# Block 0 of a four-block transformer: the norm ahead of the second expert call, taken from one place behind the attention into pieces inside it

## The chip, the cores and the metric

The kernel runs on one core of a Trainium2 chip. The engines are named as in the profile: PE multiplies matrices, DVE and ACT work element by element, POOL issues the indirect transfers, SP issues the other transfers. The metric is the device time of one launch in microseconds (us); lower is better.

## The reference, cut to what matters

`x` has 4096 tokens of 128 numbers (16 batches of 256). Four blocks follow one another, each an expert or dense layer, an attention, and the same layer again. Only block 0 is touched by the change:

```
x = x + 0.5 * experts0(layernorm(x))
x = x + attention0(layernorm(x))        # causal linear attention, 16 heads of 8
x = x + 0.5 * experts0(layernorm(x))    # the second call
```

`attention0` maps q and k through `x + 1` or `exp(x)`, and takes for each token `sum(q.k v) / (sum(q.k) + 1e-6)` over the tokens up to it, then a projection and a bias. `experts0` sends each token to the one of eight experts whose router logit is highest, so every token's logits are needed before the first expert can start.

## The kernel before, in words

The tokens lie in 32 tiles of 128: tile `j` of `x`, of the normed `xn`, and of its transpose `xnT`. Batch `b` owns tiles `2b` and `2b + 1`.

**Attention of block 0** (`attn0`). A loop runs over the 16 batches `b` and over four groups of heads `g`. In each (b, g):

- `scores` multiplies keys with queries on PE (L665, two PSUM tiles of a pool of three), and DVE masks each result (L669);
- `values` of the group two places earlier multiplies the masked scores with the values on PE (L708, and the running state at L720), and ACT copies the sums from PSUM into `u` (L730);
- at g = 0 PE and DVE build the state (L689, L699), and `recips` of batch b - 2 (L600, L601) turns the sums of the denominators into reciprocals. It stores them and loads them back spread over rows (`a_rd`, `a_den`, L602 and L604);
- at g = 1 `sums_out` of batch b - 1 sends `u` to memory and loads the numerators and denominators back (`a_ud`, `a_num`, `a_dr`, L589 to L593);
- at g = 2 `divide` of batch b - 2 (L609), at g = 3 `project_out` of it: four matmuls on PE (L617, L618) and the addition into `x` on DVE (L620);
- in even batches, at g = 0, 1 and 2, `project` makes the keys, queries and values of the next pair of batches: a matmul (L636), two activations (L638, L640), one operation on DVE (L642) and transfers into the heads' rows (L541), and for the values four times a matmul (L649) and an addition (L650). `keys_turned` (L678, L680) transposes keys.

The sums, the projections, the state, the turned keys and the transposes of a norm share a PSUM pool of two slots (`pst`, `bufs=2`), used in turn in the order of the program. A slot is free when the engine that reads it is done.

Behind the loop come the last `values`, and then, in this order, `sums_out(15)`, `recips(14)`, `divide(14)`, `project_out(14)`, `recips(15)`, `divide(15)`, `project_out(15)`.

**Order.** `pin` ties an instruction to the pinned one before it on the same engine, so most of PE's, ACT's and DVE's order is that of the program text. What is not pinned (the additions into `x`, the features, `layernorm`) is placed by a scheduler between them. Each engine works through its order without overtaking.

**The norm of before.** `ffn0(1)` begins with `layernorm()`: two halves of 16 tiles. Each takes statistics on DVE (L272, L273), an exact reciprocal square root with one activation of ACT (L254 to L262), 16 operations on DVE that write `xn` (L279), transposes on PE (L282) and copies to `xnT` on ACT (L284). The scheduler moves the statistics of a batch to just behind its addition into `x`, and the rest of the first half into batches 10 and 11 of the attention. The second half comes after the last batch. `ffn0` then stores `xn` in four transfers (L333), makes the logits (L345) and routes from L347 on.

**The norm in pieces.** Later blocks use `norm_piece(c)`: four tiles' statistics, then the reciprocal square root in Newton steps on DVE (`roots`, L292 to L306), and four activations on ACT that write `xn` (L315). `turn_piece(c)` transposes four tiles on PE (L323) and copies them on ACT (L324). All of it is pinned.

Of the kernel before, what the change touches and what calls it, by code (L numbers as in the profile page):

```python
# [9 lines left out]
F32 = mybir.dt.float32  # L10
I32 = mybir.dt.int32
U32 = mybir.dt.uint32
AF = mybir.ActivationFunctionType
# [5 lines left out]
P = 128  # L19
# [6 lines left out]
LN_EPS = 1e-5  # L26
# [45 lines left out]
def macaron_kernel(ctx: ExitStack, tc: tile.TileContext, I: dict, out: bass.AP):  # L72
    nc = tc.nc
    V, S, PE, G, SP = nc.vector, nc.scalar, nc.tensor, nc.gpsimd, nc.sync
# [4 lines left out]
    small = ctx.enter_context(tc.tile_pool(name="small", bufs=2))  # L79
    dram = ctx.enter_context(tc.tile_pool(name="dram", bufs=1, space=DRAM))  # L80
    pst = Banks()


    x = main.tile([P, NT, D], F32, name="x")
# [152 lines left out]
    def pin(ins):  # L237

        e = ins.ins.engine
        if e in pinned:  # L240
            tc.add_manual_dep(
                ins.ins,
                pinned[e],
                mybir.DependencyInfo(mybir.DependencyClass.NoSync, mybir.DependencyReason.DATA),
                reason="order of the pipeline",
            )
        pinned[e] = ins.ins.name
        return ins
# [15 lines left out]
    def layernorm(halves=(0, 1)):  # L264

        half = NT // 2
        for h in halves:
            st = small.tile([P, half, 6], F32, tag="lnst", name="ln_st")
            mv = small.tile([P, half, 2], F32, tag="lnmv", name="ln_mv")
            rstd = small.tile([P, half], F32, tag="lnr", name="ln_rstd")  # L270
            for j in range(half):
                V.bn_stats(st[:, j, :], x[:, h * half + j, :])  # L272
                V.bn_aggr(mv[:, j, :], st[:, j, :])  # L273
            rsqrt(rstd, mv[:, :, 1], LN_EPS, half, "ln")
            for c in range(0, half, 4):
                tp = pst.tile([P, 512], F32, tag="tp", name="ln_tp")
                for i in range(4):
                    k, j = c + i, h * half + c + i
                    V.tensor_scalar(  # L279
                        xn[:, j, :], x[:, j, :], mv[:, k, 0:1], rstd[:, k : k + 1], ALU.subtract, ALU.mult  # L280
                    )
                    PE.transpose(tp[:, i * P : (i + 1) * P], xn[:, j, :], ident)  # L282
                j = h * half + c
                S.copy(xnT[:, j * P : (j + 4) * P], tp)  # L284

    def roots(src, eps):


        st = small.tile([P, 4, 6], F32, tag="pst", name="ln_st")
        mv = small.tile([P, 4, 2], F32, tag="pmv", name="ln_mv")  # L290
        for j in range(4):
            pin(V.bn_stats(st[:, j, :], src[:, j, :]))  # L292
        for j in range(4):
            pin(V.bn_aggr(mv[:, j, :], st[:, j, :]))
        v = small.tile([P, 4], F32, tag="pv", name="ln_v")
        pin(V.tensor_scalar(v, mv[:, :, 1], eps, None, ALU.add))
        r = small.tile([P, 4], F32, tag="pr", name="ln_r")
        pin(V.tensor_scalar(r.bitcast(I32), v.bitcast(I32), 1, None, ALU.logical_shift_right))
        pin(V.tensor_scalar(r.bitcast(I32), r.bitcast(I32), -1.0, float(0x5F3759DF), ALU.mult, ALU.add))
        w = small.tile([P, 4], F32, tag="pw", name="ln_w")  # L300
        for k in range(3):
            pin(V.scalar_tensor_tensor(w, r, -0.5, r, ALU.mult, ALU.mult))
            pin(V.tensor_tensor(w, w, v, ALU.mult))
            pin(V.scalar_tensor_tensor(r, w, 1.5, r, ALU.add, ALU.mult))
        less = small.tile([P, 4], F32, tag="pl", name="ln_less")
        pin(V.scalar_tensor_tensor(less, mv[:, :, 0], -1.0, r, ALU.mult, ALU.mult))  # L306
        return less, r

    def norm_piece(c):

        t0 = 4 * c
        less, r = roots(x[:, t0 : t0 + 4, :], LN_EPS)
        for j in range(4):
            pin(
                S.activation(  # L315
                    xn[:, t0 + j, :], x[:, t0 + j, :], AF.Identity, bias=less[:, j : j + 1], scale=r[:, j : j + 1]
                )
            )

    def turn_piece(c):  # L320
        tp = pst.tile([P, 512], F32, tag="tp", name="ln_tp")
        for i in range(4):
            pin(PE.transpose(tp[:, i * P : (i + 1) * P], xn[:, 4 * c + i, :], ident))  # L323
        pin(S.copy(xnT[:, c * 512 : (c + 1) * 512], tp))  # L324
# [2 lines left out]
        return xnT[:, j * P : (j + 1) * P]  # L327


    def ffn0(call):  # L330
        layernorm()
        for c in range(0, NT, 8):
            SP.dma_start(  # L333
                out=xn_dram[c * P : (c + 8) * P, :].rearrange("(j p) d -> p j d", p=P), in_=xn[:, c : c + 8, :]
# [1 line left out]
        with tc.tile_pool(name=f"f0r{call}", bufs=1) as rp, tc.tile_pool(name=f"f0w{call}", bufs=3) as wp, tc.tile_pool(  # L336
# [102 lines left out]
            n = B0 // P  # L439
# [183 lines left out]
    def attn0():  # L623
        with tc.tile_pool(name="a0", bufs=2) as ap, tc.tile_pool(name="a0k", bufs=1) as bp, tc.tile_pool(
# [116 lines left out]
            for b in range(BATCH):  # L741
                us[b] = ap.tile([P, NG, SEQ], F32, tag="u", name="a0_u")
                for g in range(NG):
                    aa[b, g] = scores(b, g)
                    if b == 1 and g == 0:
                        layernorm((1,))
                    if g > 1:
                        values(b, g - 2)
                    elif b:
                        values(b - 1, g + 2)  # L750
                    if g == 0:
                        state(b)
                        if b > 1:
                            H.recips(b - 2)
                    if g == 1 and b:
                        H.sums_out(b - 1, us.pop(b - 1))
                    if g == 2 and b + 1 < BATCH and b % 2 == 0:
                        keys_turned(b + 1)
                    if g == 2 and b > 1:
                        H.divide(b - 2)  # L760
                    if g == 3 and b > 1:
                        H.project_out(b - 2)
                    if b % 2 == 0 and g < 3:
                        project(b // 2 + 1, g)
                    if g == 2 and b + 1 < BATCH and b % 2:
                        keys_turned(b + 1)
# [2 lines left out]
            values(b, 3)  # L769
            H.sums_out(b, us.pop(b))  # L770
            H.recips(b - 1)
            H.divide(b - 1)
            H.project_out(b - 1)
            H.recips(b)
            H.divide(b)
            H.project_out(b)


    def attn3():
# [884 lines left out]
    def attn2():  # L1664

        NP2 = H2 // 2
        with tc.tile_pool(name="a2", bufs=2) as ap, tc.tile_pool(name="a2w", bufs=1) as wp, tc.tile_pool(
# [205 lines left out]
            def renorm(c):  # L1873

                r = held.pop("r")
                less, rs = roots(r, 1e-5)
                for j in range(4):
                    pin(S.activation(r[:, j, :], r[:, j, :], AF.Identity, bias=less[:, j : j + 1], scale=rs[:, j : j + 1]))
                xc = x[:, 4 * c : 4 * c + 4, :]
                G.tensor_tensor(xc, xc, bc(W["a2_beta"], 1, 4), ALU.add)  # L1880
                G.tensor_tensor(r, r, bc(W["a2_gamma"], 1, 4), ALU.mult)
                G.tensor_tensor(xc, xc, r, ALU.add)
# [46 lines left out]
    def ffn3(call, last):  # L1929
# [171 lines left out]
                    turn_piece(s - 5)  # L2101

    steps = [
        lambda: (ffn0(0), later_weights()), attn0, lambda: ffn0(1),
        lambda: ffn1(0, False), attn1, lambda: ffn1(1, True),
        lambda: ffn2(0), attn2, lambda: ffn2(1),
        lambda: ffn3(0, False), attn3, lambda: ffn3(1, True),
# [112 lines left out]
```

## Time and profile before

| | us |
|---|---|
| median of 3 runs | 2972.98 |
| lowest and highest | 2961.8, 2986.62 |
| the profiled execution | 2970.45 |
| its span | 2968.8 |
| PE busy in the span | 2325.6 (78%) |
| DVE busy | 1484.8 (50%) |
| ACT busy | 1056.7 (36%) |
| attention of block 0, from about 260 to 481: PE, DVE, ACT busy | 193.08, 141.29, 57.62 |
| from 481 to 514: PE, DVE, ACT busy | 21.33, 10.30, 6.43 |

The profile is one execution. A line of its timeline gives start and length in us, the engine, the line of the kernel, what is written from what, and in brackets how long the engine was idle before it and what released it. An engine that is idle costs nothing as long as what ends last doesn't wait for it.

### The profile page before, as it was taken

How to read it: one execution, taken by the hardware profiler on the slowest of the kernel's cores; microseconds unless marked ns; L12 is line 12 of the kernel's file. 1: busy time of each engine (PE TensorE's matmuls, PEld its weight loads, DVE VectorE, ACT ScalarE, POOL GpSimd, SP SyncE). 2: the span in 40 equal slices, each digit the busy share in tenths (PEclk: the TensorE clock that was granted, in tenths of full speed). 3: DMA queues.
4: the chain of work that ended last, by engine and by line, in shares of the span. 5: the costliest groups of instructions: out<-in, count | busy, mean ns of one | idle time of the engine just before them, and what ended most of it. 6: DMA issues, size and time to landing. Idle time of an engine off the chain costs nothing. (4 is left out here: it accounts for less than half of the span.)

```text
span 2968.8 us, 45435 instructions
## 1 busy us (share of the span) xinstructions
PE 2325.6 (78%) x16713; PEld 1708.1 (58%) x16713; DVE 1484.8 (50%) x4374; ACT 1056.7 (36%) x2383; POOL 766.6 (26%) x693
## 2 busy tenths in 40 slices
PE   5884987786465656268699995576999898999999
PEld 4773555675354545145466664453777655556877
DVE  5335664434437735732235556323455566654553
ACT  1222221122114412134445442243444355664443
POOL 1551000352461054167300100675111100003111
PEclk9997897797567866566899997577999989999999
DMA  4752232454341143445400002365000012210000
GB/s 142 242 163 48 86 98 69 124 162 135 78 97 54 43 107 73 137 119 142 124 1 8 5 12 71 88 146 122 1 1 1 9 46 53 71 58 12 11 8 11
DMA packets 207908, 221.13 MB, mean 74 GB/s; under 512 B 46265, under 2 KB 172938, under 8 KB 204306
## 3 DMA queue, kind: packets, MB, share of 16 engines
q1 hardware_dynamic: 171066, 179.80, 20.0%
q0 software_dynamic: 36608, 38.31, 7.4%
q8 instruction: 135, 2.21, 0.3%
q14 instruction: 99, 0.81, 0.1%
HBM read 145.88 MB, written 63.50 MB: 71 GB/s over the span
## 5 line engine op out<-in xcount | busy, mean ns | idle before, releaser
L315 ACT ACTIVATE xn<-x,ln_less,ln_r 128x128 f32<-128x128 f32 x288 | 118.6, 482 | 397.2 <-DVE ln_less L306 351.0
L482 PE MATMUL f_h<-f_xsT,f_w 128*128 128x256 f32 x736 | 193.9, 404 | 32.9 <-ACT f_sg L484 28.1
L837 DVE TENSOR_REDUCE a_nm<-a_s 128x4 f32<-128x1024 f32 x128 | 156.4, 1224 | 99.2 <-PE a_t L833 87.8
L1596 PE MATMUL f_h<-f_xgT,f_w 128*128 128x128 f32 x768 | 158.0, 369 | 38.7 <-DVE f_xgT L1590 29.1
L456 POOL DMA_INDIRECT f_xs<-xn_dram,f_src x92 | 90.7, 985 | 371.0 <-DVE f_past L429 290.0
L485 DVE SCALAR_TENSOR_TENSOR f_hs<-f_h,f_b1s,f_sg 128x256 f32<-128x256 f32 x184 | 88.1, 483 | 187.6 <-ACT f_sg L484 97.6
L841 ACT ACTIVATE a_e<-a_t 128x512 f32<-128x512 f32 x256 | 139.0, 594 | 97.2 <-PE a_t L833 97.2
L482 PEld LDWEIGHTS f_h<-f_xsT,f_w 128*128 128x128 f32 x736 | 137.2, 202 | 61.0 <-ACT f_sg L484 34.1
L1596 PEld LDWEIGHTS f_h<-f_xgT,f_w 128*128 128x128 f32 x768 | 134.5, 264 | 63.0 <-DVE f_xgT L1590 45.6
L1600 ACT ACTIVATE f_hs<-f_h,w_f_b 128x128 f32<-128x128 f32 x384 | 109.5, 368 | 171.8 <-PE f_h L1596 150.5
L833 PE MATMUL a_t<-a_q,a_k 32*128 32x256 f32 x1024 | 166.2, 408 | 4.6 <-ACT a_e L841 4.4
L323 PE MATMUL ln_tp<-ident,xn 128*128 128x128 f32 x288 | 66.1, 339 | 130.4 <-ACT xn L315 129.7
L1631 POOL DMA_INDIRECT acc<-f_ys,f_idx x96 | 151.8, 1581 | 46.9 <-DVE f_ys L1626 26.7
L484 ACT ACTIVATE f_sg<-f_h,f_b1s 128x256 f32<-128x256 f32 x184 | 84.7, 473 | 221.0 <-PE f_h L482 180.8
L833 PE MATMUL a_s<-a_k,a_q 32*128 32x256 f32 x1024 | 153.4, 426 | 2.3 <-DVE a_nm L837 1.6
L1626 DVE TENSOR_SCALAR f_ys<-f_up,f_xg,f_share 128x128 f32<-128x128 f32 x96 | 39.3, 410 | 189.4 <-PE f_up L1623 144.2
L2016 ACT ACTIVATE f_nh<-f_c,w_f_sh 128x256 f32<-128x256 f32 x192 | 87.0, 500 | 129.4 <-DVE f_c L2035 103.8
L323 PEld LDWEIGHTS ln_tp<-ident,xn 128*128 128x128 f32 x288 | 40.3, 160 | 157.8 <-ACT xn L315 144.8
L1154 POOL DMA_INDIRECT acc<-f_ys,f_idy x64 | 100.4, 1569 | 89.0 <-DVE f_ys L1150 63.7
L503 POOL DMA_INDIRECT yt_dram<-f_ys,f_dst x92 | 90.8, 987 | 117.7 <-DVE f_ys L499 93.7
L1963 POOL TENSOR_TENSOR f_t<-f_nh 128x512 f32<-128x512 f32 x16 | 20.3, 1270 | 382.5 <-PE f_m L1997 362.9
L833 PEld LDWEIGHTS a_s<-a_k,a_q 32*128 32x128 f32 x1024 | 89.6, 195 | 45.9 <-issue 32.8
(446 smaller groups left out, 5520.8 us busy)
## 6 DMA issues: line engine op xcount, KB each, us to landing
f_w<-in_f_w SPq DMA_DIRECT2D x24, 1024.0 KB
f_w<-in_f_w SPq DMA_DIRECT2D x46, 512.0 KB
f_w<-in_f_w SPq DMA_DIRECT2D x70, 256.0 KB
a_ud<-a_u SPq DMA_DIRECT2D x32, 512.0 KB
f_wgu<-in_f_wgu SPq DMA_DIRECT2D x16, 768.0 KB
acc<-zeros SPq DMA_DIRECT2D x14, 512.0 KB
acc_t<-acc SPq DMA_DIRECT2D x28, 256.0 KB
f_wd<-in_f_wd SPq DMA_DIRECT2D x16, 384.0 KB
```

What stands on the lines that cost most here:

```text
L315: S.activation(xn[:, t0 + j, :], x[:, t0 + j, :], AF.Identity, bias=less[:, j : j + 1], scale=r[:, j : j + 1])
L323: pin(PE.transpose(tp[:, i * P : (i + 1) * P], xn[:, 4 * c + i, :], ident))
L456: G.indirect_dma_start(out=xs[:, i, :], out_offset=None, in_=xn_dram, in_offset=bass.IndirectOffsetOnAxis(ap=src[:, s : s + 1], axis=0),)
L482: pin(PE.matmul(h[:, k, :], w1[:, cc * P : (cc + 1) * P], xsT, start=True, stop=True))
L503: G.indirect_dma_start(out=yt_dram, out_offset=bass.IndirectOffsetOnAxis(ap=dst[:, s : s + 1], axis=0), in_=ys[:, i, :], in_offset=None,)
L833: pin(PE.matmul(ps[:, c, :], sta[:, c * P : (c + 1) * P], mov, start=True, stop=True))
L837: pin(V.tensor_reduce(m, sp, AX.X, ALU.max, negate=True))
L841: pin(S.activation(e, tp, AF.Exp, scale=scale))
L1154: G.indirect_dma_start(out=acc_two[e % 2], out_offset=bass.IndirectOffsetOnAxis(ap=idy[:, e : e + 1], axis=0), in_=ys[:, i, :], in_offset= ...
L1596: pin(PE.matmul(h[:, s, :], w1[:, e % GE2, s, :], xgT, start=True, stop=True))
L1600: pin(S.activation(acts[e][:, s, :], h[:, s, :], AF.Gelu, bias=W["f2_b1"][:, col : col + 1]))
L1631: G.indirect_dma_start(out=acc2[e % 2], out_offset=bass.IndirectOffsetOnAxis(ap=idx[:, e : e + 1], axis=0), in_=ys, in_offset=None, comput ...
```

## The change: norm by pieces inside the attention

`ffn0(1)` no longer begins with `layernorm()`. In its place `attn0` calls `norm_piece(b // 2 - 2)` at g = 1 of the even batches 4 to 14 (pieces 0 to 5, two batches or more behind the addition into `x`). Behind the loop, the transposes of pieces 0 to 3 and the norm of piece 6 stand between `recips(14)` and `divide(14)`; the norm of tiles 28 and 29 and the transposes of pieces 4 to 6 stand between `recips(15)` and `divide(15)`; the norm of tiles 30 and 31 and the transposes of piece 7 come last. `roots` takes a list of spans and works on two or four tiles at a time; for the later blocks it does what it did. Two tiles' scratch has tags of its own.

```diff
-    def roots(src, eps):
+    def roots(srcs, eps):
-        st = small.tile([P, 4, 6], F32, tag="pst", name="ln_st")
+        n = sum(src.shape[1] for src in srcs)
+        tag = f"p{n}"
+        st = small.tile([P, n, 6], F32, tag=tag + "st", name="ln_st")
...
-    def norm_piece(c):
+    def norm_tiles(*spans):
-        t0 = 4 * c
-        less, r = roots(x[:, t0 : t0 + 4, :], LN_EPS)
-        for j in range(4):
+        less, r = roots([x[:, lo:hi, :] for lo, hi in spans], LN_EPS)
+        for k, j in enumerate(j for lo, hi in spans for j in range(lo, hi)):
             pin(
-                S.activation(
-                    xn[:, t0 + j, :], x[:, t0 + j, :], AF.Identity, bias=less[:, j : j + 1], scale=r[:, j : j + 1]
-                )
+                S.activation(xn[:, j, :], x[:, j, :], AF.Identity, bias=less[:, k : k + 1], scale=r[:, k : k + 1])
             )
+    def norm_piece(*cs):
+        norm_tiles(*[(4 * c, 4 * c + 4) for c in cs])
...
-    def ffn0(call):
-        layernorm()
+    def ffn0(call, normed):
+        if not normed:
+            layernorm()
...
                     if g == 3 and b > 1:
                         H.project_out(b - 2)
+                    if g == 1 and b > 3 and b % 2 == 0:
+                        norm_piece(b // 2 - 2)
                     if b % 2 == 0 and g < 3:
                         project(b // 2 + 1, g)
...
             H.sums_out(b, us.pop(b))
             H.recips(b - 1)
+            for c in range(4):
+                turn_piece(c)
+            norm_piece(b // 2 - 1)
             H.divide(b - 1)
             H.project_out(b - 1)
             H.recips(b)
+            norm_tiles((2 * b - 2, 2 * b))
+            for c in range(4, 7):
+                turn_piece(c)
             H.divide(b)
             H.project_out(b)
+            norm_tiles((2 * b, 2 * b + 2))
+            turn_piece(7)
...
-        lambda: (ffn0(0), later_weights()), attn0, lambda: ffn0(1),
+        lambda: (ffn0(0, False), later_weights()), attn0, lambda: ffn0(1, True),
```

More of the change, by code (lines that the diff above doesn't have):

```diff
@@ L284, in layernorm @@
                 S.copy(xnT[:, j * P : (j + 4) * P], tp)
-    def roots(src, eps):
-        st = small.tile([P, 4, 6], F32, tag="pst", name="ln_st")
-        mv = small.tile([P, 4, 2], F32, tag="pmv", name="ln_mv")
-        for j in range(4):
-            pin(V.bn_stats(st[:, j, :], src[:, j, :]))
-        for j in range(4):
+    def roots(srcs, eps):
+        n = sum(src.shape[1] for src in srcs)
+        tag = f"p{n}"
+        st = small.tile([P, n, 6], F32, tag=tag + "st", name="ln_st")
+        mv = small.tile([P, n, 2], F32, tag=tag + "mv", name="ln_mv")
+        tiles = [src[:, j, :] for src in srcs for j in range(src.shape[1])]
+        for j, t in enumerate(tiles):
+            pin(V.bn_stats(st[:, j, :], t))
+        for j in range(n):
             pin(V.bn_aggr(mv[:, j, :], st[:, j, :]))
-        v = small.tile([P, 4], F32, tag="pv", name="ln_v")
+        v = small.tile([P, n], F32, tag=tag + "v", name="ln_v")
         pin(V.tensor_scalar(v, mv[:, :, 1], eps, None, ALU.add))
-        r = small.tile([P, 4], F32, tag="pr", name="ln_r")
+        r = small.tile([P, n], F32, tag=tag + "r", name="ln_r")
         pin(V.tensor_scalar(r.bitcast(I32), v.bitcast(I32), 1, None, ALU.logical_shift_right))
         pin(V.tensor_scalar(r.bitcast(I32), r.bitcast(I32), -1.0, float(0x5F3759DF), ALU.mult, ALU.add))
-        w = small.tile([P, 4], F32, tag="pw", name="ln_w")
+        w = small.tile([P, n], F32, tag=tag + "w", name="ln_w")
         for k in range(3):
@@ L304, in roots @@
             pin(V.scalar_tensor_tensor(r, w, 1.5, r, ALU.add, ALU.mult))
-        less = small.tile([P, 4], F32, tag="pl", name="ln_less")
+        less = small.tile([P, n], F32, tag=tag + "l", name="ln_less")
         pin(V.scalar_tensor_tensor(less, mv[:, :, 0], -1.0, r, ALU.mult, ALU.mult))
         return less, r
-    def norm_piece(c):
-        t0 = 4 * c
-        less, r = roots(x[:, t0 : t0 + 4, :], LN_EPS)
-        for j in range(4):
-            pin(
-                S.activation(
-                    xn[:, t0 + j, :], x[:, t0 + j, :], AF.Identity, bias=less[:, j : j + 1], scale=r[:, j : j + 1]
-                )
-            )
+    def norm_tiles(*spans):
+        less, r = roots([x[:, lo:hi, :] for lo, hi in spans], LN_EPS)
+        for k, j in enumerate(j for lo, hi in spans for j in range(lo, hi)):
+            pin(
+                S.activation(xn[:, j, :], x[:, j, :], AF.Identity, bias=less[:, k : k + 1], scale=r[:, k : k + 1])
+            )
+    def norm_piece(*cs):
+        norm_tiles(*[(4 * c, 4 * c + 4) for c in cs])
     def turn_piece(c):
@@ L1875, in renorm @@
                 r = held.pop("r")
-                less, rs = roots(r, 1e-5)
+                less, rs = roots([r], 1e-5)
                 for j in range(4):
```

## The prediction

> **What bounds the kernel now.** I read the page first. Its span is 2968.8 us; the busy shares name no engine as the bound of the whole, and its chain of waits has no piece before 1881 us, so for this stage I read the waits and the timeline of the stage itself. Attention of block 0 runs from 260 to 481 us, and PE is busy 193.08 of those 221 us, DVE 141.29, ACT 57.62. From 481 to the first router instruction at 513.33 a tail follows in which DMA round trips and the norm of the second half stand in a row.
>
> First view: one even batch (6) and the start of the next, in order of time (start, length, engine, line, form, and in brackets the idle time before and its releaser).
>
> ```profile
> 359.84 1.28 DVE L669 TENSOR_TENSOR a_a<-a_s,causal 128x512 f32<-128x512 f32 x2
> ...
> 361.87 0.69 DVE L642 SCALAR_TENSOR_TENSOR a_z<-a_ex,a_z 128x512 f32<-128x512 f32 x1 [0.75 <-ACT a_z L640]
> 362.14 0.33 PE L678 MATMUL a_ktp<-ident,a_z 128*128 128x128 f32 x1
> 362.32 0.37 ACT L730 COPY a_u<-a_po 128x256 f32<-128x256 f32 x1 [0.49 <-ACT a_z L640]
> 362.47 1.28 DVE L669 TENSOR_TENSOR a_a<-a_s,causal 128x512 f32<-128x512 f32 x2
> ...
> 362.75 1.16 PE L649 MATMUL a_vp<-w_a_wv,xnT 128*128 128x128 f32 x8 [0.28 <-ACT a_u L730]
> ...
> 367.08 0.73 PE L665 MATMUL a_s<-a_q,a_k 32*128 32x128 f32 x16
> ...
> 368.27 1.26 DVE L669 TENSOR_TENSOR a_a<-a_s,causal 128x512 f32<-128x512 f32 x2
> ...
> 370.56 0.18 DVE L600 TENSOR_SCALAR a_dr<-a_dr 128x32 f32<-128x32 f32 x1 [0.84 <-DMA a_dr<-a_ud]
> ```
>
> The reader is to see the small line on ACT at 362.32. That copy empties the sums of group 0 out of PSUM, and the value projection on PE waits for it (0.28 us), because `pst` has two slots: group 0's sums, the turned keys and the value projection follow one another, and the third takes the slot of the first. PE holds its written order, so what delays this copy stops PE.
>
> Second view: a `norm_piece` where nothing else is in its way, later in the same kernel.
>
> ```profile
> 2098.18 0.86 DVE L292 BATCH_NORM_STATS2 ln_st<-x 128x6 f32<-128x128 f32 x4
> 2098.97 0.36 DVE L294 BATCH_NORM_AGGREGATE ln_mv<-ln_st 128x2 f32<-128x6 f32 x4
> ...
> 2101.74 0.16 DVE L306 SCALAR_TENSOR_TENSOR ln_less<-ln_mv,ln_r 128x4 f32<-128x4 f32 x1
> ...
> 2101.94 1.65 ACT L315 ACTIVATE xn<-x,ln_less,ln_r 128x128 f32<-128x128 f32 x4 [6.94 <-DVE ln_less L306]
> ```
>
> It is a chain of 21 DVE instructions, 3.72 us from 2098.18 to 2101.90, and then 1.65 us on ACT.
>
> Third view: the tail.
>
> ```profile
> 483.07 0.18 DVE L600 TENSOR_SCALAR a_dr<-a_dr 128x32 f32<-128x32 f32 x1 [3.23 <-DMA a_dr<-a_ud]
> ...
> 487.82 0.42 DVE L609 TENSOR_TENSOR a_num<-a_num,a_den 128x256 f32<-128x256 f32 x1 [4.02 <-DMA a_den<-a_rd]
> ...
> 496.19 0.43 DVE L609 TENSOR_TENSOR a_num<-a_num,a_den 128x256 f32<-128x256 f32 x1 [3.97 <-DMA a_den<-a_rd]
> ...
> 498.95 0.42 DVE L620 TENSOR_TENSOR x<-a_y,x 128x256 f32<-128x256 f32 x1 [2.33 <-PE a_y L618]
> ...
> 500.14 0.17 DVE L254 TENSOR_SCALAR rs_v<-ln_mv 128x16 f32<-128x16 f32 x1
> ...
> 501.80 4.19 DVE L279 TENSOR_SCALAR xn<-x,ln_mv,ln_rstd 128x128 f32<-128x128 f32 x16
> ...
> 510.72 0.58 ACT L284 COPY xnT<-ln_tp 128x512 f32<-128x512 f32 x1 [4.11 <-PE ln_tp L282]
> ...
> 513.33 0.42 DVE L347 TENSOR_TENSOR f_lg<-f_lgp,w_f_rb 128x256 f32<-128x256 f32 x1 [7.34 <-issue]
> ```
>
> From the last sum into x (498.95) to the router (513.33) it takes 14.4 us, all of it norm, transposes, copies and logits of 16 tiles.
>
> **The change, part by part.** The instruction order of the changed kernel shows it. PE's order differs only in the tail. In each of steps 4, 6, 8, 10, 12 DVE has, after the masks of group 1, the statistics, aggregates and three small operations, then the q feature (L642), then ten small ones, and only then the masks of group 2. ACT has four `xn` activations before that copy of group 0's sums. Step 14 is the same without projections.
>
> *Tail, gain.* Counted from the last sums on PE, 481 on the clock of before. Before `divide` of batch 14, DVE runs piece 6: 483.7 + 3.72 = 487.4, and the divide waits for its DMA until 487.8 anyway: nothing. Batch 15's `recips` loses 0.8 us of statistics ahead of it (started 491.67): 491.05, its divide 495.6. The first pair's chain (two tiles fewer: 3.72 - 2x0.28 - 2x0.12 = 2.9 us) ends at 494.6, inside the DMA wait. But the copies of pieces 4 to 6 stand on ACT behind those two activations, piece 6's transposes need a slot from them, and batch 15's projection stands on PE behind piece 6. So: activations to 495.5, copy 496.1, four cold transposes to 497.3, projection 2.9 us (four matmuls near 0.72), sum into x 500.3 to 500.75, that is 1.4 later than now. Then 2.9 for the last pair, 0.9 for two activations, 0.5 for two transposes, 0.6 copy, 1.0 for four logits, small gaps: router at 506.7. Gain 513.33 - 506.7 = **6.6 us** (5 to 8).
>
> *Steps 4 to 12, cost.* In step 6 the statistics begin at 361.04, after the masks. Chain 3.72 and the q feature 0.69 in its midst: `less` ends at 365.45. Four activations to 367.15, the copy to 367.5, value projection at 367.55 in place of 362.75: **4.8 us** of PE stall. (DVE itself: group 2's masks end at 366.6, no later than PE wants them.) PE stands idle some 5 us, and its clock follows. The rows: after the DMA waits of odd steps, which leave PE idle 1.6 to 2.9 us, sixteen L665 take 1.24 us in place of 0.73 for the next 3.5 to 7 us. The Trainium skill (TensorE: Matmul & The Clock Gate, Part 1) has half clock only after an idle window of about 3.4 us, and full clock after a busy one as long. By the rule a stall costs 3.4 x (1 - 1/1.7) = 1.4 us; by the rows some 5 us cold, 2.1. I take the row's 2.1; both put a penalty on this stall, and they part on step 14, whose gaps are 2.1 and 1.0 us. Nothing at the one end, 3.3 (all of the 4.3 us of work to 367.08 cold) at the other.
>
> What takes from it: the statistics no longer stand ahead of the next masks (PE was done at 367.81, masks began 368.27: 0.4); the wait for the sums' DMA at L600 fills up (0.73, 0.84, 1.36, 0 and 0.51 in the five odd steps; 0.8 taken, the zero being beside the large norm that goes); SP issues three `a_q` before the reciprocals' store (0.3). SP is not delayed otherwise: q's first issue, 364.26, is after the delayed feature, 363.4. Behind L600 the round trip to the divide (6 us, of which 3.3 is idle DVE) moves along whole; it hides nothing. Net 4.8 + 2.1 - 0.4 - 0.8 - 0.3 = 5.4; five of them **27.0 us** (3.5 to 8 each).
>
> *Step 14.* Statistics from 464.3, `less` 468.0, activations to 469.7, copy 470.1; group 1's sums start at 470.15 in place of 466.66: 3.5, plus 1.0 of clock (rule 0, row 2.1), less 0.4 and 0.8: **3.3 us**.
>
> *What goes.* The large norm of the first half (16 `xn` at 337 ns and the square root) ran in steps 10 and 11. That pair took 26.83 us (406.60 to 433.43) against 26.4 (353.78 to 380.22): **0.4 us** gained. Two loads of ACT's tables went beside other work: nothing.
>
> *DMA.* The same four 0.5 MB stores of `xn`, but three inside the attention and in other places on SP. The one ahead of a `den` at 424.0 raised its wait to 4.43 us from 3.3 to 3.9: **0.8 us** for the new one in step 7. The one after step 14 has landed before the next reciprocals are stored. The last is covered by 30 us of routing (513 to the first gather at 544). POOL's order is unchanged, and the wait for its gathers moves with the router.
>
> Sum: -6.6 + 27.0 + 3.3 - 0.4 + 0.8 = **+24.1 us**. The profiled execution took 2970.45 (span 2968.8 and 1.65 around it); the median of the three runs, 2972.98, is 2.5 above. 2970.45 + 24.1 = 2994.6, on the median 2997; I say **2996**.
>
> **Rivals.** *It hides, and the tail counts.* For it: the large norm, 7 us of DVE, cost only 0.4 us; the DVE idles 4 to 5 us in an even step. Then 2970.45 - 6.6 = 2964, faster by 0.2%. Against it: that norm was spread into the idle stretches (5, 7, 2 and 2 tiles between masks), and put nothing on ACT ahead of a copy. It decides if the `xn` activations get done before PE needs the copy at 362.3. 12 in 100.
>
> *The clock stays low into the odd step.* All 4.3 us behind the stall cold (3.3), another 1.5 before L600, 8.1 net a step: 40.5, and 5 for step 14; -6.6 + 40.5 + 5 + 0.4 = +39, **3010**. For it: a cold stretch of 7 us (350.6 to 357.8) after only 2.0 us of idling. Against: others of 3.5 us. It decides where cold runs past 367. 20 in 100.
>
> *The order isn't as said,* and a scheduler puts the norm elsewhere: the built order excludes it. What remains is an effect that no row shows: 3 in 100 for a gain of over 1%.
>
> **How the numbers follow.** Forecast 65 in 100, its own range 2984 to 3007 (3.5 to 7 a step). The range 2972 to 3014 adds the cold rival and leaves out the hidden one and a little above. About 1% (30 us) is what a measurement of this kernel tells from no change: the three runs spread by 0.8%. Within 1%: the hidden rival and 43 of the forecast's 65; slower: 20 from the cold rival and 22 of the forecast's upper end.
>
> **What would show it.** Right: in six even steps an idle of 4 to 5 us on PE ahead of L649's new line, released by `a_u`, with ACT's four `xn` just before; low PE clock after it; pairs of steps of 31 to 33 us in place of 26.4; attention's last sums near 511; 25 to 26 us from there to the router in place of 32. Wrong: pairs near 26.4, or the masks of group 2 as what PE waits for; a tail that gives back less than 5 us; a change in any stage after the router.

## The result, and the profile after

The changed kernel takes 2997.17 us (median of 11 runs, 2978.42 to 3010.89), the kernel before in the same comparison 2971.8 us (11 runs). The ratio is 1.0066, interval 1.0045 to 1.0088: within 1%, but a real loss. The forecast was 2996. The profiled execution took 2992.51 us with a span of 2990.8, that is 22.0 more than the span of before.

The whole difference lies in one stage, and one event bounds it at each end: batch 0's state mask on DVE (L699, now L703) and the first addition of the router's logits (L347, now L351). In what follows "the stage" is the time from the one to the other. It took 231.74 us before (281.59 to 513.33) and takes 257.14 (278.00 to 535.14): **25.4 more**. From the router to the end it is 2455.5 us before and 2455.7 after. What runs ahead of the stage came 3.6 us earlier in the profile of after; nothing is changed there, and that is why the spans differ by less than the stage.

The first view is the timeline of step 6 and the start of step 7 in the kernel after (start, length, engine, line, form; idle before it and its releaser).

```profile
361.71 0.86 DVE L295 BATCH_NORM_STATS2 ln_st<-x 128x6 f32<-128x128 f32 x4
...
363.37 0.69 DVE L646 SCALAR_TENSOR_TENSOR a_z<-a_ex,a_z 128x512 f32<-128x512 f32 x1
...
365.75 0.16 DVE L309 SCALAR_TENSOR_TENSOR ln_less<-ln_mv,ln_r 128x4 f32<-128x4 f32 x1
365.82 1.28 DVE L673 TENSOR_TENSOR a_a<-a_s,causal 128x512 f32<-128x512 f32 x2
365.94 1.65 ACT L317 ACTIVATE xn<-x,ln_less,ln_r 128x128 f32<-128x128 f32 x4 [3.44 <-DVE ln_less L309]
...
367.49 0.35 ACT L734 COPY a_u<-a_po 128x256 f32<-128x256 f32 x1
...
367.90 2.08 PE L653 MATMUL a_vp<-w_a_wv,xnT 128*128 128x128 f32 x8 [4.75 <-ACT a_u L734]
...
373.98 0.73 PE L669 MATMUL a_s<-a_q,a_k 32*128 32x128 f32 x16
...
376.27 0.17 DVE L604 TENSOR_SCALAR a_dr<-a_dr 128x32 f32<-128x32 f32 x1
```

Read it from the bottom up. PE stood 4.75 us ahead of the value projection and was released by the copy of group 0's sums. That copy stood behind four `xn` activations, which had ACT waiting 3.44 us for `less`, the last of the DVE chain. In the kernel before, the same projection waited 0.28 us. Its eight matmuls now take 2.08 us in place of 1.16: PE comes out of the stall at a low clock. The last line has no bracket: the wait for the sums' transfer (0.84 us before) is gone.

The waits view of steps 4 to 14 gives the whole (what PE waited for at which line; us in total, times, longest).

```profile
PE a_vp L653 <- ACT a_u L734: 23.9, 5, 4.8
PE a_y L622 <- DVE a_num L613: 12.7, 5, 4.3
PE a_s L669 <- DVE a_a L673: 2.4, 1, 2.4
```

Before, the first of these three was 1.4 us in all, the second 10.6 and the third 2.6.

The third view is the windows of single steps (stretch; length, then busy time of PE, PEld, DVE, ACT, POOL; granted clock of PE (1.00 is full speed), DMA share, GB/s). First the kernel before, steps 6, 7 and 9; then the kernel after, the same.

```profile
355.99:369.44 13.45, 13.17 (x201) 7.88 (x205) 8.95 (x20) 4.18 (x9) 0.00 (x0) 0.94 0.28 80
369.44:382.19 12.75, 10.28 (x173) 6.48 (x166) 7.28 (x19) 1.63 (x5) 0.00 (x0) 0.87 0.31 89
...
394.94:408.45 13.51, 10.04 (x174) 6.21 (x167) 7.70 (x21) 3.35 (x8) 0.00 (x0) 0.89 0.29 85
```

```profile
356.92:376.06 19.14, 14.39 (x193) 9.05 (x197) 11.55 (x38) 5.70 (x13) 0.00 (x0) 0.79 0.24 72
376.06:391.13 15.07, 11.00 (x178) 7.05 (x178) 6.50 (x13) 1.67 (x6) 0.00 (x0) 0.81 0.30 90
...
410.21:421.13 10.92, 9.23 (x178) 5.82 (x178) 6.50 (x13) 1.68 (x6) 0.00 (x0) 0.93 0.26 77
```

The even step is 5.7 us longer. The odd step 9 is 2.6 shorter, with PE busy for less time at a higher clock; but the odd step 7 is 2.3 longer. Step 7 holds a store of `xn`, shown here by three lines of the timeline (SPq is the queue of SP):

```profile
378.45 0.51 SPq L337 DMA_DIRECT2D xn_dram<-xn  x1
379.05 1.15 SPq L608 DMA_DIRECT2D a_den<-a_rd  x1
...
385.00 0.43 DVE L613 TENSOR_TENSOR a_num<-a_num,a_den 128x256 f32<-128x256 f32 x1 [5.45 <-DMA a_den<-a_rd]
```

Last the tail. The last sums are copied at 508.93:

```profile
513.74 0.42 DVE L613 TENSOR_TENSOR a_num<-a_num,a_den 128x256 f32<-128x256 f32 x1 [0.59 <-DMA a_den<-a_rd]
517.14 0.42 DVE L624 TENSOR_TENSOR x<-a_y,x 128x256 f32<-128x256 f32 x1 [2.98 <-PE a_y L622]
...
526.65 0.42 DVE L624 TENSOR_TENSOR x<-a_y,x 128x256 f32<-128x256 f32 x1 [4.30 <-PE a_y L622]
...
535.14 0.42 DVE L351 TENSOR_TENSOR f_lg<-f_lgp,w_f_rb 128x256 f32<-128x256 f32 x1 [4.75 <-PE f_lgp L349]
```

From the last sum into `x` (526.65) it is 8.5 us to the router, where it was 14.4. From the last copy it is 26.2, where it was 32.4.

### The profile page after: what moved, and what is told of

Same layout as the page of the kernel before. It is cut to its first block, busy times and chain, and to the rows that moved or that the text cites. A ratio compares the mean times of both kernels' runs of the same rounds, so it can differ in the third digit from the quotient of the medians.

```text
span 2990.8 us, 45523 instructions
## 1 busy us (share of the span) xinstructions
PE 2332.5 (78%) x16713; PEld 1707.1 (57%) x16713; DVE 1493.2 (50%) x4447; ACT 1066.9 (36%) x2410; POOL 767.8 (26%) x693
## 3 DMA queue, kind: packets, MB, share of 16 engines
q1 hardware_dynamic: 171066, 179.80, 19.8%
## 5 line engine op out<-in xcount | busy, mean ns | idle before, releaser
L317 ACT ACTIVATE xn<-x,ln_less,ln_r 128x128 f32<-128x128 f32 x320 | 132.0, 483 | 435.8 <-DVE ln_less L309 398.7
L1611 PE MATMUL f_h<-f_xgT,f_w 128*128 128x128 f32 x768 | 151.4, 358 | 38.0 <-DVE f_xgT L1605 26.9
L326 PE MATMUL ln_tp<-ident,xn 128*128 128x128 f32 x320 | 72.5, 338 | 136.1 <-ACT xn L317 131.3
L848 PE MATMUL a_t<-a_q,a_k 32*128 32x256 f32 x1024 | 173.4, 424 | 4.7 <-ACT a_e L856 4.7
L486 PEld LDWEIGHTS f_h<-f_xsT,f_w 128*128 128x128 f32 x736 | 136.5, 200 | 62.0 <-ACT f_sg L488 32.9
L848 PEld LDWEIGHTS a_t<-a_q,a_k 32*128 32x128 f32 x1024 | 107.0, 195 | 20.8 <-ACT a_e L856 13.4
```

The lines of the kernel that those rows point to most:

```text
L317: S.activation(xn[:, j, :], x[:, j, :], AF.Identity, bias=less[:, k : k + 1], scale=r[:, k : k + 1])
L486: pin(PE.matmul(h[:, k, :], w1[:, cc * P : (cc + 1) * P], xsT, start=True, stop=True))
L848: pin(PE.matmul(ps[:, c, :], sta[:, c * P : (c + 1) * P], mov, start=True, stop=True))
L1611: pin(PE.matmul(h[:, s, :], w1[:, e % GE2, s, :], xgT, start=True, stop=True))
```

## The experiments

The runs were made on several chips; each ratio is against the kernel before on the same chip (medians of before: 2913.5 for e1 to e5, 2968.6 for e6, e10 and the two repeats, 2914.6 for e11, e13 and e14, 2915.4 for e12). The table has one traced execution of each. "4 to 14" is the stretch from batch 4's to batch 15's state mask: its length, PE's busy time, its idle time (the difference), and its granted clock. "Tail" runs from the last copy of sums to the router.

| kernel | 4 to 14 | PE busy | PE idle | clock | tail | stage | ratio |
|---|---|---|---|---|---|---|---|
| before | 142.2 | 126.6 | 15.6 | 0.90 | 32.4 | 231.7 | |
| b_again | 142.1 | 127.8 | 14.3 | 0.89 | 32.7 | 236.3 | |
| after | 173.6 | 133.9 | 39.6 | 0.81 | 26.2 | 257.1 | 1.0066 [1.0045, 1.0088] |
| a_again | 176.7 | 136.6 | 40.1 | 0.81 | 26.0 | 260.7 | |
| e1_split | 166.7 | 144.1 | 22.7 | 0.79 | 28.5 | 252.9 | 1.0071 [1.0049, 1.0092] |
| e3_odd | 148.8 | 132.9 | 15.9 | 0.85 | 28.3 | 239.1 | 1.0006 [0.9988, 1.0023] |
| e4_store | 170.8 | 137.9 | 32.9 | 0.81 | 26.0 | 252.4 | 1.0065 [1.0039, 1.0092] |
| e5_loop | 178.5 | 142.8 | 35.7 | 0.79 | 30.7 | 267.1 | 1.0083 [1.0056, 1.0110] |
| e6_tail_alone | 143.3 | 126.5 | 16.9 | 0.89 | 28.4 | 233.6 | 1.0000 [0.9981, 1.0018] |
| e10_idle | 160.0 | 141.3 | 18.7 | 0.80 | 26.2 | 242.7 | 1.0035 [1.0014, 1.0056] |
| e13_dve | 150.5 | 135.3 | 15.2 | 0.85 | 30.6 | 237.1 | 1.0027 [1.0010, 1.0045] |
| e14_act | 142.1 | 127.8 | 14.4 | 0.89 | 30.6 | 230.1 | 1.0002 [0.9981, 1.0023] |
| e11_idles | 141.3 | 127.7 | 13.6 | 0.89 | 26.1 | 222.4 | 0.9980 [0.9964, 0.9996] |
| e12_order | 138.1 | 124.4 | 13.6 | 0.93 | 26.6 | 218.8 | 0.9983 [0.9965, 1.0002] |

**The two kernels once more: b_again, a_again.** Unchanged, for the spread of the stage from one execution to the next.

> The kernel before, once more, for its trace on this chip. If the stage is steady, batch 0's state mask to the router takes 229 to 235 us (231.7 in the first trace) and even and odd steps pair to 25.5 to 27 us; the rival is that one execution's granted clock moves the stage by 10 us or more, and then the stage lengths of single traces, 239 against 253, say little.

> The changed kernel, once more, for its trace on this chip. If the stage is steady it takes 253 to 260 us (257.1 in the first trace), with six idles of 4 to 5 us ahead of the value projection or the next sums, and the steps that hold a store of xn ahead of a den (7 and 11) 4 to 6 us longer than the other odd ones. The rival is a spread of 10 us or more from one execution to the next.

The stage repeats to 4.6 us in the kernel before and to 3.5 in the kernel after, and 4 to 14 to 0.1 and 3.1. So differences of 8 us and more in the table can be read, and smaller ones hardly. The step with the widest spread in a_again is step 10, at 21.7 us in place of 19.6; the section on the hardware comes back to it.

**The loop half alone: e5_loop.** Pieces 0 to 3 in steps 4 to 10 as in the change; the second half by the old `layernorm((1,))` behind the loop.

```diff
-        if not normed:
-            layernorm()
+        layernorm((1,) if normed else (0, 1))
...
-                    if g == 1 and b > 3 and b % 2 == 0:
+                    if g == 1 and 3 < b < 12 and b % 2 == 0:
...
```

> One part of the change alone: norm_piece 0 to 3 in steps 4 to 10 and the transposes of these pieces, as in the changed kernel; the second half is normed by layernorm behind the attention, as before. Theory (costs sit in the even steps, the gain in the tail): steps 4 to 11 cost what they do in the changed kernel (23 us together with two stores), the tail is that of before, 41.7 us from batch 15's state mask: stage about 255 us. Rival (the pieces are hidden, and something in steps 12 to 15 or the tail made the loss): stage 231 to 236 us.

The loss is there without the new tail, and with only four pieces in the loop. Steps 4 to 11 took 34.2 us more than before, in the kernel after 23.4 more. Most of the 10.8 between the two lies in steps 6, 8 and 10 with the same stall of PE: 21.5 to 21.7 us each, as in step 10 of a_again, where the kernel after has 19.1 to 19.6. Each of them has a stretch of 13.7 us at low clock in place of 6.8 (see the section on the hardware).

**The tail half alone: e6_tail_alone.** No piece in steps 4 to 14; the first half by the old norm, pieces 4 and 5 in step 15 and behind it, the rest of the tail as in the change.

```diff
-                    if g == 1 and b > 3 and b % 2 == 0:
-                        norm_piece(b // 2 - 2)
+                    if b == BATCH - 1 and g == 2:
+                        norm_piece(4)
...
             H.sums_out(b, us.pop(b))
+            norm_piece(5)
             H.recips(b - 1)
-            for c in range(4):
-                turn_piece(c)
+            layernorm((0,))
             norm_piece(b // 2 - 1)
```

> Only the tail of the change: no piece of the norm in the loop up to step 14; the first half is normed by the old large norm (which runs in steps 10 and 11 as before), piece 4 stands in step 15 ahead of batch 13's divide, piece 5 ahead of batch 14's reciprocals, the rest of the tail as in the changed kernel. Theory A (the whole loss is made in steps 4 to 14, the tail is a pure gain): steps 4 to 14 as in the kernel before (pairs near 26.4 us), 25 to 28 us from the last sums to the router in place of 32.4, the stage from batch 0's state mask to the router near 227 us in place of 231.7, a ratio of 0.998. Rival B (the tail's gain depends on the first half being normed ahead, which frees DVE and PE there): 30 us or more from the last sums to the router, ratio 1.000 or above. Rival C (a norm chain of DVE in step 15 costs what it cost in an even step): the stretch from batch 15's state mask to the last sums grows from 9.4 us to 14 or more, and the gain is gone.

Rival C. Steps 4 to 14 are those of before and the tail is 4 us shorter, but the stretch from batch 15's state mask to the last copy grew from 9.4 (12.3 in b_again) to 15.4 us. The timeline of step 15 shows it happen:

```profile
472.86 0.86 DVE L295 BATCH_NORM_STATS2 ln_st<-x 128x6 f32<-128x128 f32 x4
...
476.49 1.28 DVE L673 TENSOR_TENSOR a_a<-a_s,causal 128x512 f32<-128x512 f32 x2
...
477.69 0.41 DVE L624 TENSOR_TENSOR x<-a_y,x 128x256 f32<-128x256 f32 x1
478.16 1.08 PE L712 MATMUL a_po<-a_a,a_va 128*32 128x128 f32 x16 [3.85 <-DVE x L624]
478.17 0.35 ACT L734 COPY a_u<-a_po 128x256 f32<-128x256 f32 x1
```

The chain of one piece stands on DVE ahead of the last masks and of an addition into `x`; its activations stand on ACT ahead of the copy of group 1's sums. PE, at the next sums, waits 3.85 us. What released it is the addition, which ended at 478.1; the copy ended only at 478.5, when PE had begun. So it is work on DVE behind the chain that PE waited for here, and not the copy.

**The stores: e4_store.** The changed kernel with one store of all of `xn` at the end, in place of four on the way.

```diff
+        n_st = NT if normed else 8
-        for c in range(0, NT, 8):
+        for c in range(0, NT, n_st):
```

> The changed kernel with one store of all of xn at the end in place of four, so that none stands on SP in the attention. Theory (the stores of steps 7 and 11 hold up the denominators' load by some 3.4 us each): steps 7 and 11 fall from 15.1 and 15.3 us to 11.5, stage about 250 us. Rival (those two odd steps are longer for another reason, the clock or the projections): they stay at 15, stage 257 us.

Steps 7 and 11, which hold a store in the kernel after, fell from 15.07 and 15.31 us to 9.39 and 9.38. The divide of step 7 waits 2.09 us for its denominators, no longer 5.45:

```profile
368.54 0.42 DVE L614 TENSOR_TENSOR a_num<-a_num,a_den 128x256 f32<-128x256 f32 x1 [2.09 <-DMA a_den<-a_rd]
```

So those two steps are 5.7 and 5.9 us longer with a store ahead of a `den`, not 0.8. In step 7 some 3.3 us of that are idle time of PE and 2.4 busy time at the lower clock (0.81 against 1.00). Yet the ratio did not move: steps 4 and 12 took 21.8 and 21.7 us in place of 19.1, at a granted clock of 0.71 in step 4, and of the 11.6 us only 2.8 are left in the stretch. That is not the price of taking the stores away: step 4 comes before the first of them, and steps as long stand in e5_loop and a_again, which have the stores. With an interval from 1.0039 to 1.0092, the ratio can't tell what the stores cost the whole launch.

**The activations off the copy: e1_split.** DVE's chain (`norm_roots`) stays in its place; the four activations (`norm_write`) stand behind the copies of group 0's sums and of the turned keys.

```diff
...
+                    if g == 2 and b > 3 and b % 2 == 0:
+                        norm_write(*held_norm)
...
                     if g == 1 and b > 3 and b % 2 == 0:
-                        norm_piece(b // 2 - 2)
+                        c = b // 2 - 2
+                        held_norm = norm_roots((4 * c, 4 * c + 4))
```

> Read by the stage from the first state mask of the attention (a_sm of batch 0) to the first router instruction (f_lg): 231.7 us before, 257.1 after. The Newton chain stays on DVE at g = 1 of the even steps; only the four xn activations move on ACT, behind the copies of group 0's sums and of the turned keys. Theory (the copy waits on ACT behind the activations, and PE for the copy): the 4.8 us idle ahead of the value projection goes; what is left is a wait of some 2 us for the masks of group 2, too short to cool the clock, less the 1.5 us that the next step gives back: stage about 237 us, time about 20 us below the changed kernel. Rival (the chain of 21 instructions on DVE ahead of the masks is what costs): the stage stays within 3 us of 257.

The stage came out 4 us below the kernel after, near the rival's figure and 16 above the theory's. The copy is early again and the value projection waits 0.28 us, but the even steps 4 to 12 still take 17.2 to 18.3 us. PE in step 6 of e1_split, from its timeline:

```profile
345.85 1.16 PE L664 MATMUL a_vp<-w_a_wv,xnT 128*128 128x128 f32 x8 [0.28 <-ACT a_u L745]
346.94 0.49 PE L680 MATMUL a_s<-a_q,a_k 32*128 32x128 f32 x4
348.99 0.71 PE L680 MATMUL a_s<-a_q,a_k 32*128 32x128 f32 x12 [1.56 <-DVE a_a L684]
...
352.87 1.24 PE L680 MATMUL a_s<-a_q,a_k 32*128 32x128 f32 x16
...
356.22 1.24 PE L680 MATMUL a_s<-a_q,a_k 32*128 32x128 f32 x16
```

Two things take the stall's place. Group 3's scores wait 1.56 us for group 2's masks, which stand behind the chain on DVE. And PE then runs at the low clock from 351.3 to 358.1, although it is never idle there: the 1.56 us, expected to be too short to lower the clock, were not. Over 4 to 14 the idle time falls by 17 us against the kernel after, and the busy time rises by 10.

**ACT alone: e14_act.** The kernel before, with four activations that wait for nothing in the place of the `xn` ones.

```diff
+                    if g == 1 and b > 3 and b % 2 == 0:
+                        dt = ap.tile([P, P], F32, tag="dose", name="dose")
+                        for k in range(4):
+                            pin(S.activation(dt, x[:, 4 * (b // 2 - 2) + k, :], AF.Identity))
```

> The kernel before, with nothing but four activations of 128x128 on ACT (into a scratch tile) in steps 4, 6, 8, 10, 12 and 14, in the place of the xn activations but waiting for nothing: they stand ahead of the q feature's activations and of the copy of group 0's sums, 1.65 us of ACT. Theory A: the q feature and that copy come about 1.2 us later, PE waits 1 to 2 us ahead of the value projection, and the low clock behind it makes 3 to 5 us of each such step; ratio 1.005 to 1.009. Rival B (only the stall counts): 1 to 2 us a step, ratio 1.001 to 1.003. Rival C (ACT has slack enough, and the copy alone never was the matter): no step grows by more than 0.5 us.

Rival C: nothing. The 1.3 us that these four take on ACT fit between its other work. What hurt in the kernel after was that they wait for `less` with the copy behind them.

**DVE alone: e13_dve.** The kernel before, with twelve small copies on DVE in the place of the chain.

```diff
+                    if g == 1 and b > 3 and b % 2 == 0:
+                        dt = small.tile([P, 4], F32, tag="dose", name="dose")
+                        for k in range(12):
+                            pin(V.tensor_copy(dt, x[:, 4 * (b // 2 - 2), :4]))
```

> The kernel before, with nothing but twelve small copies (4 columns each, into a scratch tile) on DVE behind group 1's masks in steps 4, 6, 8, 10, 12 and 14, ahead of the q feature and of group 2's masks: some 2 us of DVE. Theory A (a short stall of PE is worth several times its length, since the granted clock stays low behind it): PE waits 0.5 to 1.5 us for group 2's masks, and the even steps grow by 3 to 5 us; stage 248 to 262 us, ratio 1.005 to 1.009. Rival B (only the stall itself counts): even steps grow by 0.5 to 1.5 us, stage below 242 us, ratio 1.000 to 1.003.

Rival B by its numbers: PE waited 5.8 us for masks in all (2.6 before), and 4 to 14 grew by 8.3 us. The growth is uneven: steps 4 and 6 by next to nothing, step 8 by 0.8, steps 10 and 12 by 1.6 and 1.7, step 14 by 1.4 to 3.1. Some 2 us of DVE about use up the slack in front of those masks; the chain's 3.7 exceed it.

**The chain earlier in the even step: e10_idle.** DVE's chain right behind the reciprocals, the activations behind the copies as in e1_split, one store.

```diff
...
                             H.recips(b - 2)
+                        if b > 3 and b % 2 == 0:
+                            c = b // 2 - 2
+                            held_norm = norm_roots((4 * c, 4 * c + 4))
...
```

> The pieces of the first half stay in the even steps, but DVE's chain stands right behind the reciprocals, where DVE idles 2.5 us before the first feature, and not behind group 1's masks; ACT's four activations stand behind the copies of group 0's sums and of the turned keys; one store of xn at the end. Theory A (what costs is the place: a chain of 3.7 us ahead of masks and of a copy that PE waits for at once): about 1.3 us of the chain is not covered, so even steps grow by 1 to 2.5 us, no idle over 1 us ahead of the value projection, stage 228 to 238 us against 231.7 before, ratio 0.999 to 1.002. Rival B (any such chain in an even step puts PE at a lower granted clock, wherever it stands): even steps grow by 4 to 6 us as in the other kernels, granted clock in steps 4 to 14 near 0.80 in place of 0.90, stage near 252 us, ratio 1.007.

The stage lies between A and B, the clock is B's 0.80, and the even steps take 14.4 to 19.1 us. PE in step 6 of e10_idle:

```profile
354.75 0.49 PE L681 MATMUL a_s<-a_q,a_k 32*128 32x128 f32 x4
356.70 0.71 PE L681 MATMUL a_s<-a_q,a_k 32*128 32x128 f32 x12 [1.47 <-DVE a_a L685]
...
359.11 2.08 PE L665 MATMUL a_vp<-w_a_wv,xnT 128*128 128x128 f32 x8
361.12 1.24 PE L681 MATMUL a_s<-a_q,a_k 32*128 32x128 f32 x16
...
366.77 1.24 PE L681 MATMUL a_s<-a_q,a_k 32*128 32x128 f32 x16
...
370.12 1.24 PE L681 MATMUL a_s<-a_q,a_k 32*128 32x128 f32 x16
372.33 0.73 PE L681 MATMUL a_s<-a_q,a_k 32*128 32x128 f32 x16
```

A single stall of 1.47 us, for group 1's masks this time, and behind it 13.6 us at the low clock (357.9 to 371.6) with PE busy for all but 0.1 of them. The step is 5.6 us longer than before: a quarter of that is the stall, the rest the clock. Steps 10 and 12, with stalls of 1.33 and 1.25 us, have no low stretch behind them and took 15.1 us each.

**The chain in the odd steps: e3_odd.** The chain ahead of the divide of steps 5 to 15, where DVE waits for `den`, the activations behind the copy of the turned keys, one store.

```diff
...
+                    if g == 2 and b > 3 and b % 2:
+                        c = b // 2 - 2
+                        held_norm = norm_roots((4 * c, 4 * c + 4))
                     if g == 2 and b > 1:
                         H.divide(b - 2)
...
```

> The pieces 0 to 5 move from the even steps to the odd ones 5 to 15: the chain on DVE ahead of divide, where DVE idles 3.3 us for a DMA, the activations on ACT behind the turned keys' copy; and all of xn is stored in one transfer at the end. Theory: both engines are idle there, so the pieces cost 0 to 0.5 us each and the tail's gain stays: stage about 228 us (226 to 232), 4 us under before, ratio to before 0.998 to 1.000. Rival (a norm inside the attention costs wherever it stands, by DVE time or by the clock): stage 240 us or more.

Most of the loss is gone: 148.8 us for 4 to 14. But the stage is longer than was expected of it. What keeps it from a gain is steps 9 and 11 (15.7 and 16.0 us; before 13.5 and 13.8) and step 15 with the tail, 42.3 us from the state mask to the router against 35.2 in the kernel after.

**The chain cut to fit: e11_idles.** Statistics, aggregates and three small operations (`norm_stats`) behind the reciprocals of an even step; the other ten (`norm_rest`) behind the last masks of that step; the activations behind its last copy; one store.

```diff
...
                             H.recips(b - 2)
+                        if b > 3 and b % 2 == 0:
+                            c = b // 2 - 2
+                            held_norm = norm_stats(4 * c, 4 * c + 4)
...
+                    if g == 3 and b > 3 and b % 2 == 0:
+                        norm_rest(*held_norm)
                     if g == 3 and b > 1:
                         H.project_out(b - 2)
...
```

> The pieces of the first half are cut so that DVE works them in stretches where it idles in the kernel before: statistics, aggregates and three small operations right behind the reciprocals of an even step (2.5 us idle there), the ten others behind the last masks of that step (1.1 us idle, and the large norm's statistics are gone from the next), so that no masks that PE waits for stand behind them; the activations follow on ACT behind the last copy of the step; one store of xn at the end. Theory A (the loss comes from what PE waits for behind the chain: each stall, however short, is followed by a long stretch at a low granted clock): no stall, steps 4 to 14 as in the kernel before within 1 us, 26 us from the last sums to the router, stage 225 to 230 us against 231.7 and 236.3 in the two traces of before, ratio 0.997 to 0.999. Rival B (more work on DVE and ACT lowers the granted clock whether PE waits or not): granted clock in steps 4 to 14 near 0.80, stage above 240 us, ratio 1.003 or more.

Theory A's figures, and rival B is out (though "however short" is too much: the stalls of 1.3 us in e10_idle had no low stretch behind them). DVE is busy 98.1 us in 4 to 14, as in the kernel after (99.9), ACT 39.2 (40.1), and the clock is 0.89. The timeline of step 6 in e11_idles:

```profile
332.77 0.81 DVE L319 BATCH_NORM_STATS2 ln_st<-x 128x6 f32<-128x128 f32 x4
...
335.81 1.28 DVE L704 TENSOR_TENSOR a_a<-a_s,causal 128x512 f32<-128x512 f32 x2
...
338.30 0.37 ACT L765 COPY a_u<-a_po 128x256 f32<-128x256 f32 x1 [0.49 <-ACT a_z L675]
338.45 1.28 DVE L704 TENSOR_TENSOR a_a<-a_s,causal 128x512 f32<-128x512 f32 x2
...
338.73 1.16 PE L684 MATMUL a_vp<-w_a_wv,xnT 128*128 128x128 f32 x8 [0.28 <-ACT a_u L765]
...
344.09 0.16 DVE L336 SCALAR_TENSOR_TENSOR ln_less<-ln_mv,ln_r 128x4 f32<-128x4 f32 x1
...
344.29 1.65 ACT L339 ACTIVATE xn<-x,ln_less,ln_r 128x128 f32<-128x128 f32 x4 [2.38 <-DVE ln_less L336]
```

The copy's bracket reads 0.49 and the projection's 0.28, the very numbers of the kernel before. The median is 2907.7 us against 2914.6: with the loop's loss gone, the tail's gain is what is left. This is the one kernel of the table whose whole interval lies below 1, and only just.

**The tail's order: e12_order.** As e11_idles, with the transposes of pieces 4 to 6 ahead of the norm of tiles 28 and 29.

```diff
             H.recips(b)
-            norm_tiles((2 * b - 2, 2 * b))
             for c in range(4, 7):
                 turn_piece(c)
+            norm_tiles((2 * b - 2, 2 * b))
```

> The kernel of e11_idles with one line moved in the tail: pieces 4 to 6 are turned before the pair of batch 14 is normed, so that their copies on ACT don't stand behind the two activations of that pair and batch 15's projection on PE not behind piece 6. By the prediction's working of the tail this is worth 1.4 us (24.7 from the last sums to the router in place of 26.1). Steps 4 to 14 as in e11_idles: near 142 us from batch 4's to batch 15's state mask, where the changed kernel took 173.6 and 176.7. Ratio 0.996 to 0.999 if e11_idles's 0.998 holds on another chip; the rival is that it was drawn low, and the ratio is 0.999 to 1.001.

The ratio of e11_idles held on another chip, 2908.2 against 2915.4, with an interval that just touches 1. The 1.4 us did not come; the tail took 26.6. Another piece of work slid into the opened place: the logits' matmuls, which the scheduler puts where it likes, stand between the two matmuls of batch 15's projection.

```profile
463.76 3.58 PE L380 MATMUL f_lgp<-w_f_rw,xnT 128*128 128x8 f32 x16
467.20 0.77 PE L653 MATMUL a_y<-w_a_wo,a_num 128*128 128x128 f32 x2
```

The numerators were ready at 464.1, and the projection took them up 3.1 us later.

## Why the prediction was right, point by point

The sum was +24.1 and the stage grew by 25.4. With a spread of some 4 us from one execution to the next, a match that close is in part luck, as are the terms below that cancelled. By place: steps 0 to 3 +0.5, steps 4 to 13 +25.5 (forecast 27.0 - 0.4 + 0.8 = 27.4), step 14 +5.9 (3.3), step 15 and tail -6.5 (-6.6).

- **The stall** was right in mechanism and place, and nearly in size: 23.9 us over five steps, 4.78 each, of which 0.28 were there before; so 4.5 were added, forecast 4.8. e14_act shows that ACT's work without the wait costs nothing, and e1_split that the stall goes when the activations leave the front of the copy: it is the wait for `less` there.
- **"DVE itself: group 2's masks end at 366.6, no later than PE wants them"** was true only as long as the copy held PE up as well. e1_split took the copy away, and the masks were what PE waited for. The forecast stood because it never took the stall apart; a reader who had repaired the stall by moving the activations alone, on the strength of that sentence, would have gained nothing.
- **The clock** was mis-sized. The stretch from the value projection to the next batch's first scores took 6.08 us against 4.33: 1.75 for the stall, between the row's 2.1 and the prediction's estimate of 1.4 from the Trainium skill (TensorE: Matmul & The Clock Gate, Part 1). The upper end, 3.3 us for 4.3 us of work all cold, should read 3.0 by the prediction's own factor of 1.7. But net it is far less: in steps 4 to 13 PE's busy time grew by 4.5 us in all (117.0 to 121.5), not by 5 x 2.1 = 10.5. The even step's PE is busy 1.2 us longer in step 6, while that of the odd steps without a store is 1.5 us less on average (11.0, 10.0 and 11.0 us before, 9.5, 9.2 and 8.7 after).
- **The odd steps** give back more than was counted: steps 5, 9 and 13 are 2.0, 2.6 and 3.6 us shorter, forecast 0.8 for the wait at the old L600. That wait did vanish (it had been 0.73, 1.36 and 0.51 in these three); the rest is the clock just named and shorter waits of PE.
- **The store** was the largest miss: 0.8 us for the new one in step 7, by e4_store 5.7 us in that step (and 5.9 in step 11, which had a store before too). The two errors, odd steps and stores, have opposite signs and by luck cancelled: the odd steps together changed by -4.3 us, forecast -3.6 (-4.0 for the waits, +0.8 and -0.4).
- **Pairs of steps** were to take 31 to 33 us. They took 30.6, 34.2, 30.0, 34.9 and 28.4 from step 4 on, 31.6 on average: those with a store above, the others below.
- **Step 14** cost 5.9 us in place of 3.3, and the mechanism was the wrong one. The stall ahead of the copy that the sum had, 3.5 us, measured 0.6. The second part of group 3's scores waited 2.4 us for masks (the third line of the waits view) and the next sums 0.6 for the copy, and the clock was low from 491.3 on (0.72 in the window of the step, 0.92 before). It is the mask wait, which the prediction had excluded, seen once in the kernel after itself. And it is where the prediction's rule and row parted: 10.2 us of low clock followed, so the rule's 0 for a gap of this length was wrong.
- **The tail** with step 15 was right to 0.1 us in size, again by luck: this stretch differs by 3.3 us between the two traces of before. And two errors cancelled. The x sum of batch 15 came 17.7 us behind the last copy, forecast 19.3; from it to the router it was 8.5 us, forecast 6.4. The last logits, counted as four matmuls of 1.0 us, are eight and take 1.88.

Of the rivals, "it hides" is refuted by after and e5_loop, and the order was as said. The rival of a low clock into the odd step did not come about in the kernel after, whose odd steps ran at 0.90 to 1.00 where no store stood; it is what e1_split and e10_idle ran into.

## What to carry to other kernels

Where an engine works in written order, look for idle time of the engine that is to take the work and, in the same breath, for what stands next behind that place: a chain of 3.7 us in front of masks cost 2 to 6 us a step wherever it stood in an even step, and nothing over the whole stretch once it was cut in two, with the larger part behind the last masks. Moving the one wait that the profile names may only uncover the next (copy, then masks, then clock), so list all consumers behind the new work before choosing its place. And weigh the transfers that move with it: in its own step, a half-megabyte store in front of a small load that PE's next work waits for made about as much difference as the stall, though the time of the launch did not show it. A stall is priced from several traces and not from one: the same stall made steps of 18.2 to 21.8 us.

## What the runs showed of the hardware that was not expected

- **The length of a low stretch does not follow the length of the stall.** Inside the attention of these traces the granted clock is 1.00 or 0.50, and every stretch at 0.50 up to the last copy of sums lasts 3.4, 6.8, 10.2 or 13.7 us: one to four times 3.4. Three low stretches, all at the same stall of 4.75 us in step 6 (columns as in the third view): the kernel after, e5_loop and a_again.

```profile
364.97:371.78 6.81, 3.88 (x40) 3.32 (x40) 3.63 (x10) 2.06 (x6) 0.00 (x0) 0.50 0.45 128
...
350.27:363.91 13.64, 13.27 (x140) 9.08 (x144) 5.42 (x11) 1.22 (x5) 0.00 (x0) 0.50 0.11 31
...
367.72:371.10 3.38, 3.28 (x28) 2.83 (x32) 0.69 (x1) 0.21 (x2) 0.00 (x0) 0.50 0.18 49
```

  What differs is when the clock fell. The same stall, 4.6 to 4.9 us long, stands ahead of the value projection 19 times in the traces of after, a_again, e4_store and e5_loop, and the low stretch goes with the moment of the fall:

| clock fell, from the start of the stall | low stretch | length of the step | times |
|---|---|---|---|
| 1.74 to 2.62 us | 6.8 us | 19.1 to 19.8 us | 10 |
| 3.29 to 4.45 us | 13.7 us | 21.5 to 21.8 us | 6 |
| 4.55 to 4.63 us | 3.4 us | 18.2 to 18.4 us | 3 |

  In step 6 of the kernel after, 2.9 of the 6.8 us pass while PE still stands idle; behind a short stall nearly all of the low stretch falls on work. So a short stall can cost more clock than a long one. The stall of 1.47 us in e10_idle was followed by 6.8 us in step 4 and by 13.7 in steps 6 and 8, the ones of 1.33 and 1.25 by none. Over 4 to 14, the added waits for masks were 7.8 us in e1_split, 7.4 in e10_idle and 3.2 in e13_dve (10.4, 10.0 and 5.8 against 2.6), and the stretch grew by 24.5, 17.8 and 8.3 us: 2.4 to 3.1 times the wait (e1_split still has the stores). In the kernel after it was 31.4 us for 25.0 of added waits on copy, masks and numerators, 1.3 times. Why the moment of the fall matters, and how it is set, stays open: the rule of the Trainium skill that the prediction weighs (TensorE: Matmul & The Clock Gate, Part 1), an idle window of about 3.4 us to lower the clock and as long a busy one to raise it, has the unit of these stretches, but explains neither the fall behind stalls of 1.5 us nor 13.6 us at low clock with PE busy. Here the traces decide.
- **A store ahead of a load on one queue.** Behind a store of `xn`, the load of the denominators took 1.15 us to issue in step 7 of the kernel after, without it 0.59 in e4_store, and the wait at its consumer was 5.45 us against 2.09.
